# The first tree's masks by matrix products instead of a trip through DRAM, in a six-layer kernel on one core

## The chip, the cores and the metric

The kernel runs on one core of a Trainium2 chip. TensorE (PE) multiplies matrices, VectorE (DVE), ScalarE (ACT) and GpSimd (POOL) work on rows of 128 partitions, and SyncE (SP) does nothing but issue DMAs; ACT issues a few as well. Each engine runs its own list of instructions in order and waits on semaphores for the others. The time is the device time of one execution in microseconds: 1149.53 us, the median of three runs (1147.91 to 1149.95).

## The reference, cut to what matters

The input x holds 4 rows (batches) of 512 tokens with 128 features. Six layers follow each other, each with its own normalisation and a residual: a tree layer, causal attention with 16 heads, the tree layer again with the same weights, a mixture of 8 experts, a state-space block, and the mixture again. The change touches the first tree layer:

```python
x = x + 0.5 * _L0_ffn_ref(_layernorm(x, axis=-1), ...)

def _fff(x, node_w, node_b, w1, b1, w2, b2):     # once each for q, k and v
    for _ in range(DEPTH):                       # 4 levels, 16 leaves
        score = jnp.einsum('nd,nd->n', xf, node_w[cur]) + node_b[cur]
        cur = 2 * cur + 1 + (score >= 0).astype(jnp.int32)
    sel = jax.nn.one_hot(cur - N_NODES, N_LEAVES)
    hidden = jax.nn.relu(einsum('nd,ldh->lnh', xf, w1) + b1[:, None, :])
    hidden = hidden * sel.T[:, :, None]
    return einsum('lnh,lho->no', hidden, w2) + sel @ b2
```

Every token goes down a tree of 15 nodes and lands in one of 16 leaves; only that leaf's 64 hidden units count. The kernel computes all 1,024 hidden units of a tree for all tokens and multiplies them by a mask of 0 and 1. The three trees give q, k and v of an attention without heads over the 512 tokens of the row.

## The kernel before, in words

**Order of the work.** The table TIMES gives each job (layer letter and row: T0 to T3 are the first tree layer of rows 0 to 3, h0 to h3 the heads, and so on) due times for its preparation, its main part and its end. A loop takes the next step of the job that is due first; this gives the program order. A job that needs another one finishes that one first. The Tile framework then orders each engine's instructions itself, by the program order and its own estimate of when operands are ready, so an instruction without open operands can come long before its place in the program. Each role of tiles has a number of buffers (BUFS for SBUF, BANKS for the 8 banks of PSUM).

**A tree layer of one row.** `tree_prep` takes the statistics of the row's four blocks of 128 tokens (`stats`: L284 bn_stats and L286 bn_aggr for each block, then some 11 small DVE operations, L294, L271 to L277 three times over, L302, that make a reciprocal root; two of their operands lie in a PSUM bank of the role tree_tr). `layer_norm` applies them, on ACT for row 0 of the first layer (L310), else on POOL (L312). `features` turns the result around on PE (L318) and splits it into a rounded high part xh (ACT, L326) and a low part xl (DVE, L327); products of three partial matmuls (`mm3`, L173 to L175) then keep nearly full precision. The node scores become bits (DVE, L350), one matmul with the matrix leafpath (L353) counts the wrong turns on the way to each leaf, and "count equals 0" gives the one-hot choice: as bytes in `taken` (L355) and as numbers in `sel` (L369).

**Masks.** A chunk is 128 hidden units, two leaves of 64; a tree has 8 chunks. The mask of a tree is a tile of 128 partitions x 8 x 512 bytes in which each leaf's row of `taken` stands 64 times. It comes by DRAM: SP writes `taken` to the tensor fff_taken (L357), and after that has landed, two DMAs for each tree (L363) read the rows back, repeated. The role mask has 2 buffers.

**Main part.** `tree_main` runs over 24 chunks n (three trees of 8): three matmuls into a bank tree_mm (or start, for the odd chunks of row 0's first tree), one DVE operation L394 that adds the bias, cuts at zero and multiplies by the mask, and five chunks later the second matmul into tree_acc (L404, two instructions of TensorE for one product in full precision). L407 adds the leaf biases by `sel`. For row 0 the weights of the three trees are loaded and split on the way (`split_tree`): a stage DMA (L166), a rounded copy on ACT (L161), the remainder on DVE (first tree) or POOL (L162). `second_bias` (L230 to L240) folds the first bias into the second. The other rows fetch the split weights from DRAM.

**Around it.** `late_loads` (five attention weights, each a stage tile and an L161 and L162) is first in the program order. `head_consts` makes the constant rows of the heads: four stacks q_bias and two stacks k_bias of 128 x 1024, set to 1 by POOL (L480), then 24 rows overwritten from DRAM (L483, L484). Later `head_stack` and `head_maxima` move the q and k rows and the maxima of one pair of row and head group into the rows 24 to 127 of a stack of queries. `head_scores` runs over a quarter of the heads: a matmul (L557) and a DVE reduction (L565) for every tile.

Of the kernel before, what the change touches and what calls it, by code (L numbers as in the profile page):

```python
# [15 lines left out]
F32 = mybir.dt.float32  # L16
F32R = mybir.dt.float32r
# [4 lines left out]
ALU = mybir.AluOpType  # L22
AX = mybir.AxisListType

P = 128
B, S, D = 4, 512, 128
# [3 lines left out]
LEAVES, LEAF_W, DEPTH = 16, 64, 4  # L30
NODES = LEAVES - 1
NCH = LEAVES * LEAF_W // P
# [80 lines left out]
def macaron(ctx: ExitStack, tc: tile.TileContext, t: dict, stages: int = 6):  # L113
    nc = tc.nc
# [6 lines left out]
    def bank(role):  # L121
        return psum.tile([P, S], F32, tag=role, name=role, bufs=BANKS[role])
# [4 lines left out]
    def tiny(shape, tag, bufs=2):  # L127

        n = int(np.prod(shape[1:]))
        if tag not in turns:  # L130
            first = taken_of[0]
            taken_of[0] += bufs * n
            assert taken_of[0] <= SCRATCH
            turns[tag] = cycle([scratch[:, first + n * i : first + n * i + n] for i in range(bufs)])
        out = next(turns[tag])
        if len(shape) == 2:
            return out
        names = "abcd"[: len(shape) - 1]
        sizes = dict(zip(names, shape[1:]))
        return out.rearrange(f"p ({' '.join(names)}) -> p {' '.join(names)}", **sizes)  # L140

    def work(role, shape=(S,), dtype=F32):

        return wp.tile([P, *shape], dtype, tag=role, name=role, bufs=BUFS[role])
# [44 lines left out]
    x = [rows[:, b] for b in range(B)]  # L189
# [12 lines left out]
    leafpath, ident_h, future_t = (whole[:, ts(k, P)] for k in range(3))  # L202
    future = whole[:, 3 * P :]


    at = {}
    col = 0
# [59 lines left out]
    def inverse_root(out, v, s):  # L267

        shape = list(out.shape)
        y = tiny(shape, f"root_{shape[1]}", 4)  # L270
        nc.vector.tensor_scalar(  # L271
            y.bitcast(I32), v.bitcast(I32), -0.5, float(0x5F3759DF), ALU.mult, ALU.add
        )
        for k in range(3):
            nc.vector.scalar_tensor_tensor(s, y, -0.5, v, ALU.mult, ALU.mult)
            nc.vector.tensor_mul(s, s, y)
            nc.vector.scalar_tensor_tensor(out if k == 2 else y, s, 1.5, y, ALU.add, ALU.mult)  # L277

    def stats(b, role, square=False):

        st = tiny([P, NT, 6], "bn", 4)
        mv = tiny([P, NT, 2], "mv", 4)
        for i in range(NT):
            nc.vector.bn_stats(st[:, i, :], x[b][:, i, :])  # L284
        for i in range(NT):
            nc.vector.bn_aggr(mv[:, i, :], st[:, i, :])  # L286
        n = 2 if square else 1
        rstd, shift = (tiny([P, n, NT], f"{r}_{n}", 4) for r in ("rstd", "shift"))

        ps = bank(role)  # L290
        var, step = (
            ps[:, k * n * NT : (k + 1) * n * NT].rearrange("p (n t) -> p n t", n=n) for k in range(2)
        )
        nc.vector.tensor_scalar_add(var[:, 0, :], mv[:, :, 1], EPS)  # L294
        if square:

            nc.vector.scalar_tensor_tensor(
                var[:, 1, :], var[:, 0, :], EPS, mv[:, :, 1], ALU.mult, ALU.add
            )
        inverse_root(rstd, var, step)  # L300
        mean = mv[:, :, 0].unsqueeze(1).to_broadcast([P, n, NT])
        nc.vector.scalar_tensor_tensor(shift, mean, -1.0, rstd, ALU.mult, ALU.mult)  # L302
        return [(rstd[:, k, :], shift[:, k, :]) for k in range(n)]

    def layer_norm(b, rstd, shift, on_act=False, role="ln"):
        ln = work(role)
        for i in range(NT):
            out, by, to = ln[:, ts(i, P)], rstd[:, i : i + 1], shift[:, i : i + 1]
            if on_act:
                nc.scalar.activation(out, x[b][:, i, :], AF.Identity, scale=by, bias=to)  # L310
            else:
                nc.gpsimd.tensor_scalar(out, x[b][:, i, :], by, to, ALU.mult, ALU.add)  # L312
        return ln
# [25 lines left out]
        return tuple(w), second_weights(k)  # L339

    def tree_prep(b, st):
        ln = layer_norm(b, *stats(b, "tree_tr")[0], st.call == 0)
        yield
        st.xn = xn = features(ln, "tree_tr")
        yield

        ps = bank("tree_tr")
        mm3(ps, nodes, xn)
        bits = work("bits", dtype=BF16)
        nc.vector.tensor_scalar(bits, ps, at["node_b"], 0.0, ALU.add, ALU.is_ge)  # L350
        yield
        ps = bank("tree_tr")
        nc.tensor.matmul(ps, lhsT=leafpath, rhs=bits, start=True, stop=True)  # L353
        taken = work("taken", dtype=U8)[:ALL_LEAVES]
        nc.vector.tensor_scalar(taken, ps[:ALL_LEAVES], 0.0, None, ALU.is_equal)  # L355
        rows = t["fff_taken"][st.call]
        nc.sync.dma_start(out=rows, in_=taken)  # L357
        st.masks = []
        for k in range(TREES):
            mask = work("mask", (NCH, S), U8)  # L360
            pairs = rows[k * LEAVES : (k + 1) * LEAVES].rearrange("(c l) s -> l c s", l=2)
            for m in range(2):
                nc.sync.dma_start(  # L363
                    out=mask[m * LEAF_W : (m + 1) * LEAF_W],
                    in_=pairs[m : m + 1].to_broadcast([LEAF_W, NCH, S]),
                )
            st.masks.append(mask)
        st.sel = work("sel", dtype=F32R)
        nc.vector.tensor_scalar(st.sel, ps, 0.0, None, ALU.is_equal)  # L369

    def tree_main(b, st):
        xn = st.xn
# [101 lines left out]
    def head_consts():  # L474

        qs, ks = [], []
        for n, lst, name in ((4, qs, "q_bias"), (2, ks, "k_bias")):
            for u in range(n):
                stack = work(name, (2, S), F32R)
                nc.gpsimd.memset(stack.bitcast(F32), 1.0)  # L480
                for g in range(2):
                    raw = work("bias")
                    nc.sync.dma_start(out=raw[:R_HH], in_=t[name][u % 2, g])  # L483
                    nc.scalar.copy(stack[:R_HH, g, :], raw[:R_HH])  # L484
                lst.append(stack)

        vv = work("vv", (2, NT, V_COLS))
        nc.gpsimd.memset(vv, 0.0)
        by_head = vv[:, :, :, : HEADS * (HD + 1)].rearrange("p m n (h c) -> p m n h c", h=HEADS)
        for m in range(2):  # L490
            nc.gpsimd.memset(by_head[:, m, :, :, HD:], 1.0)
        return qs, ks, (vv, by_head)

    def head_prep(b, st, consts):
        all_qs, _, (_, by_head) = consts()
        st.qs = all_qs[b % 2 * 2 : b % 2 * 2 + 2]
        ln = layer_norm(b, *stats(b, "head_tr")[0])

        nc.gpsimd.tensor_add(x[b], x[b], out_b.unsqueeze(1).to_broadcast([P, NT, D]))
# [667 lines left out]
def _constants():  # L1167

    f = np.float32
# [46 lines left out]
    for q in range(GROUPS):  # L1216
# [10 lines left out]
        "lower": np.broadcast_to(lower, (P, EXPERTS, EXPERTS)),  # L1227
        "state_w": np.concatenate([np.zeros((P, 6, P), f), gather.reshape(P, 1, P)], axis=1),
        "spread": spread.reshape(P, GROUPS * P),
    }, head  # L1230


# [99 lines left out]
```

## Time and profile before

| what | value |
|---|---|
| median of three runs | 1149.53 us |
| profiled execution | 1150.85 us, span 1149.1 us |
| PE busy | 1080.6 us (94%) |
| DVE busy | 909.7 us (79%) |
| ACT, POOL busy | 517.1 us (45%), 411.6 us (36%) |
| PE busy in 0 to 12, 12 to 24, 24 to 29 us | 0.17, 10.15, 0.51 us |
| PE busy in 29 to 60 us | 31.0 us |
| PE busy in 200 to 400 us | 199.88 of 200 us |
| PE busy in 800 to 900 us | 85.76 of 100 us |

The profile is of one execution; it lists for each engine the busy time, and its views give the instructions in order of time, the waits with their releasers, and the chain of work that ended last. L with a number is a line of the kernel. A PE that is busy throughout can still be slow: the granted clock is listed beside it.

### The profile page before, as it was taken

To read this page: it belongs to the slowest core of one execution; us is meant where nothing else is said; L and a number is where in the kernel's file an instruction comes from. 1 tells how busy PE (TensorE), PEld (TensorE's weight loads), DVE (VectorE), ACT (ScalarE), POOL (GpSimd) and SP (SyncE) were. 2 spreads that over 40 slices of the span, in tenths; PEclk is the share of its full clock that TensorE was granted. 3 is DMA by queue.
4 is the path that set the end of the run, shared out by engine and by line. 5 is a ranking of instruction groups with operands and counts; after the bars stand their busy time and mean duration, and the time that the engine had idled before them with its cause. 6 is when DMAs were issued, how large, how long until landed. Compare 5 with 4: busy or idle time off the path is not lost.

```text
span 1149.1 us, 16519 instructions
## 1 busy us (share of the span) xinstructions
PE 1080.6 (94%) x5536; PEld 715.5 (62%) x5536; DVE 909.7 (79%) x2199; ACT 517.1 (45%) x1078; POOL 411.6 (36%) x396
## 2 busy tenths in 40 slices
PE   3999999999999999999999999998798989998998
PEld 2666566566665667765566676675276656655677
DVE  5566787577676677776789998799989999999864
ACT  2221423233332455544533643565476567454444
POOL 4115322002100141320314651266626656656623
PEclk9999999999999999999999999999899999999999
DMA  7787755231442122333752334662038323823310
GB/s 208 203 248 215 260 137 122 75 94 57 85 139 60 54 58 60 104 85 112 232 181 90 125 84 122 234 210 92 1 98 278 127 60 125 292 74 124 111 51 10
DMA packets 79653, 146.42 MB, mean 127 GB/s; under 512 B 7537, under 2 KB 39665, under 8 KB 79569
## 3 DMA queue, kind: packets, MB, share of 16 engines
q1 hardware_dynamic: 79280, 145.07, 42.1%
q8 instruction: 44, 0.72, 0.3%
q14 instruction: 41, 0.33, 0.1%
q10 hardware_dynamic: 288, 0.30, 0.1%
HBM read 125.35 MB, written 13.70 MB: 121 GB/s over the span
## 4 chain that ended last, share of the span: by engine, by line
PE 63%; DVE 20%; issue 6%; DMA 4%; POOL 3%; ACT 3%; SPq 1%; POOLq 0%; ACTq 0%; DVEq 0%
PE tree_acc L404 11%; PE moe_acc L773 7%; DVE states L972 6%; PE head_acc L601 5%; PE tree_mm L173 4%; PE head_max L557 4%; PE head_sc L633 3%; PE moe L173 3%; PE tree_mm L175 3%; PE tree_mm L174 3%; DVE states L971 3%; PE moe L174 3%; PE moe L175 3%; DVE u L759 2%; PE state_acc L934 2%
## 5 line engine op out<-in xcount | busy, mean ns | idle before, releaser
L973 POOL TENSOR_TENSOR states<-states,cs 128x512 f32<-128x512 f32 x128 | 163.4, 1282 | 161.9 <-DVE states L972 93.1
L404 PE MATMUL tree_acc<-full,ring 128*128 128x512 f32 x384 | 194.3, 598 | 5.2 <-DVE full L394 4.9
L565 DVE CUSTOM_DVE_ANT_0 head_max<-head_max,kept 128x128 f32<-128x128 f32 (+3 forms) x256 | 126.8, 496 | 64.1 <-PE head_max L557 61.9
L394 DVE SCALAR_TENSOR_TENSOR full<-tree_mm,kept,mask 128x512 f32<-128x512 f32 x188 | 138.5, 746 | 40.2 <-PE tree_mm L175 35.1
L649 ACT ACTIVATE pt<-head_sc 128x512 f32<-128x512 f32 (+1 forms) x176 | 95.0, 559 | 139.0 <-PE head_sc L641 138.3
L972 DVE TENSOR_TENSOR_SCAN states<-decay,states 128x512 f32<-128x512 f32 x128 | 154.6, 1216 | 0.5
L773 PEld LDWEIGHTS moe_acc<-ring,u 128*128 128x128 f32 x1152 | 141.4, 193 | 17.6 <-DVE u L765 3.0
L773 PE MATMUL moe_acc<-ring,u 128*128 128x128 f32 x1152 | 145.7, 278 | 1.0 <-DVE u L759 0.7
L173 PE MATMUL moe<-xl,ring 128*128 128x512 f32 x288 | 128.8, 448 | 8.9 <-DVE u L765 1.9
L784 POOL TENSOR_TENSOR kept<-kept,y 128x512 f32<-128x512 f32 x64 | 83.4, 1303 | 136.2 <-ACT y L783 118.8
L970 ACT ACTIVATE decay<-dts,kept 128x512 f32<-128x512 f32 x128 | 88.4, 693 | 88.1 <-DVE states L972 66.5
L758 ACT ACTIVATE u<-moe 128x512 f32<-128x512 f32 x144 | 86.3, 602 | 70.4 <-PE moe L175 66.5
L759 DVE SCALAR_TENSOR_TENSOR u<-u,moe 128x512 f32<-128x512 f32 x144 | 97.0, 677 | 23.4 <-ACT u L758 23.1
L174 PE MATMUL moe<-xh,ring 128*128 128x512 f32 x288 | 115.4, 401 | 0.0
L175 PE MATMUL moe<-xh,ring 128*128 128x512 f32 x288 | 115.0, 400 | 0.0
L541 POOL TENSOR_SCALAR km<-k_bias,kept 128x512 fp32r<-128x512 f32 x64 | 43.3, 697 | 171.3 <-PE head_sc L633 151.0
L783 ACT ACTIVATE y<-moe_acc,scratch 128x128 f32<-128x128 f32 x256 | 73.3, 370 | 65.6 <-PE moe_acc L773 64.8
L173 PE MATMUL tree_mm<-xl,ring 128*128 128x512 f32 x188 | 96.1, 514 | 0.4 <-DVE full L394 0.2
L404 PEld LDWEIGHTS tree_acc<-full,ring 128*128 128x128 f32 x384 | 71.0, 190 | 35.8 <-issue 17.3
L173 PEld LDWEIGHTS moe<-xl,ring 128*128 128x128 f32 x288 | 54.8, 190 | 60.4 <-DVE u L765 10.4
L557 PE MATMUL head_max<-km,q_bias 120*128 120x512 f32 (+2 forms) x192 | 91.7, 479 | 0.5 <-POOL km L541 0.4
L971 DVE TENSOR_TENSOR states<-state_b,dtxs 128x512 f32<-128x512 f32 x128 | 85.6, 682 | 5.5 <-PE state_acc L934 2.6
(242 smaller groups left out, 1982.3 us busy)
## 6 DMA issues: line engine op xcount, KB each, us to landing
ring<-moe_parts SPq DMA_DIRECT2D x72, 512.0 KB
ring<-tree_parts SPq DMA_DIRECT2D x42, 512.0 KB
ring<-in_fff_w SPq DMA_DIRECT2D x24, 512.0 KB
mask<-fff_taken SPq DMA_DIRECT2D x48, 256.0 KB
ring<-in_moe_w SPq DMA_DIRECT2D x16, 512.0 KB
dts<-state_rows SPq DMA_DIRECT2D x32, 256.0 KB
dtxs<-state_rows SPq DMA_DIRECT2D x32, 256.0 KB
moe_parts<-moe_w SPq DMA_DIRECT2D x9, 512.0 KB
```

The source lines that it names most:

```text
L173: nc.tensor.matmul(ps, lhsT=lh, rhs=rl, start=start, stop=False)
L174: nc.tensor.matmul(ps, lhsT=ll, rhs=rh, start=False, stop=False)
L175: nc.tensor.matmul(ps, lhsT=lh, rhs=rh, start=False, stop=stop)
L394: nc.vector.scalar_tensor_tensor(full, ps, neg_b1[:, n : n + 1], st.masks[k][:, c, :], ALU.max, ALU.mult)
L404: nc.tensor.matmul(acc, lhsT=weights[k][1][:, c, :], rhs=h, start=(c == 0), stop=False)
L557: nc.tensor.matmul(view, lhsT=qs[:R_MAX, g, ts(i, P)], rhs=km[j0 // 2][:R_MAX, j0 % 2 : j0 % 2 + each, :kw], start=True, stop=True,)
L565: nc.vector.tensor_tensor_reduce(view[:, n, :], view[:, n, :], future[:, S - kw :], -1.0, float(np.finfo(np.float32).max), ALU.add, ALU.mi ...
L759: nc.vector.scalar_tensor_tensor(u, u, 1.0, ps1, ALU.add, ALU.mult)
L773: nc.tensor.matmul(acc[:, ts(i, P)], lhsT=h[c][:, ts(i, P)], rhs=w2[:, e % 4 * 2 + c, :], start=(c == 0), stop=(c == 1),)
L971: nc.vector.tensor_mul(h, bs, dtx[:, g, :])
L972: nc.vector.tensor_tensor_scan(h, dA, h, 0.0, ALU.mult, ALU.add)
L973: nc.gpsimd.tensor_mul(h, h, cs[:, q])
```

## The change

- The mask of the first tree of row 0's first layer (call 0, tree 0) no longer comes by DRAM. A matrix leaf_rows of 16 x 1024, in which leaf l has ones over its 64 hidden units, is loaded by a DMA on ACT's queue at the start and rounded by a copy on ACT. For each of the 8 chunks one matmul of its 128 columns with the first 16 rows of `sel` gives the 128 x 512 mask in a bank tree_tr, and an ACT copy writes it as bytes. The two mask DMAs of that tree go; `taken`, its DRAM tensor and the masks of the other trees and rows stay. Both new tiles have the role stage.
- In call 0 `sel` is made before `taken`, in the other calls after, as it was.
- In the first layer of rows 1 to 3 the first bn_stats instruction is held, by `keep_in_program_order`, behind the instruction that precedes it on DVE in the program order. The other three bn_stats of a row are not held; all that needs the first one follows it.
- The four stacks q_bias are no longer set to 1 by POOL; the two stacks k_bias still are.

```diff
+    raw_rows, leaf_rows = (work("stage", [NCH * P], dt)[:LEAVES] for dt in (F32, F32R))
+    nc.scalar.dma_start(out=raw_rows, in_=t["leaf_rows"])
+    nc.scalar.copy(leaf_rows, raw_rows)
...
-    def stats(b, role, square=False):
+    def stats(b, role, square=False, late=False):
...
-            nc.vector.bn_stats(st[:, i, :], x[b][:, i, :])
+            first = nc.vector.bn_stats(st[:, i, :], x[b][:, i, :])
+            if late and i == 0:
+                tc.keep_in_program_order(first)
...
-        ln = layer_norm(b, *stats(b, "tree_tr")[0], st.call == 0)
+        ln = layer_norm(b, *stats(b, "tree_tr", late=0 < st.call < B)[0], st.call == 0)
...
+        st.sel = work("sel", dtype=F32R)
+        if st.call == 0:
+            nc.vector.tensor_scalar(st.sel, ps, 0.0, None, ALU.is_equal)
         taken = work("taken", dtype=U8)[:ALL_LEAVES]
         nc.vector.tensor_scalar(taken, ps[:ALL_LEAVES], 0.0, None, ALU.is_equal)
...
             mask = work("mask", (NCH, S), U8)
+            st.masks.append(mask)
+            if st.call == 0 and k == 0:
+
+                for c in range(NCH):
+                    ps_c = bank("tree_tr")
+                    nc.tensor.matmul(
+                        ps_c, lhsT=leaf_rows[:, ts(c, P)], rhs=st.sel[:LEAVES], start=True, stop=True
+                    )
+                    nc.scalar.copy(mask[:, c, :], ps_c)
+                continue
...
-            st.masks.append(mask)
-        st.sel = work("sel", dtype=F32R)
-        nc.vector.tensor_scalar(st.sel, ps, 0.0, None, ALU.is_equal)
+        if st.call:
+            nc.vector.tensor_scalar(st.sel, ps, 0.0, None, ALU.is_equal)
...
-                nc.gpsimd.memset(stack.bitcast(F32), 1.0)
+                if lst is ks:
+                    nc.gpsimd.memset(stack.bitcast(F32), 1.0)
...
+        "leaf_rows": np.kron(np.eye(LEAVES, dtype=f), np.ones((1, LEAF_W), f)),
```

## The prediction

> **What bounds the kernel now.** I read the page first: TensorE (PE) is busy 94% of the span, 31.0 of 31 us from 29 to 60 us and 199.88 of 200 us from 200 to 400 us. So where PE stands idle early, and nothing else is late, the end should move by nearly the same time. The waits of PE from 11 to 60 us name the two large ones:
>
> ```profile
> PE tree_tr L318 <- ACT ln L310: 11.8, 1, 11.8
> PE tree_acc L404 <- DVE full L394: 4.9, 1, 4.9
> ```
>
> (us in total, times, longest). The second is this change's place. The chain of work, in order of time (start, us, what), goes through it:
>
> ```profile
> 18.77 0.24 PE tree_tr L353
> 19.03 0.70 DVE taken L355
> 19.75 0.34 SPq L357
> 21.43 0.69 SPq L363
> 22.16 5.41 DMA mask<-fff_taken
> 27.69 0.76 DVE full L394
> 28.49 2.08 PE tree_acc L404 x2
> 33.51 2.58 PE tree_acc L404 x6
> 36.08 0.46 PE tree_mm L173 x2
> ```
>
> From the choice (19.03) to the first masked chunk (27.69) 8.7 us go into DRAM and back. PE has filled its six banks with chunks 0 to 5 and done the second bias by 23.55, then stands 4.94 us; tree 1 starts at 36.08. The windows (busy us per engine, granted clock, DMA share, GB/s) add that the pause also slows what follows it:
>
> ```profile
> 24.00:29.00 5.00, 0.51 (x1) 0.50 (x2) 2.50 (x9) 0.72 (x2) 1.78 (x4) 0.95 1.08 221
> 30.00:32.00 2.00, 2.00 (x5) 1.32 (x4) 1.84 (x4) 1.05 (x1) 0.79 (x1) 0.52 1.03 283
> ```
>
> The granted clock is 0.52 there. Between 28.49 and 32.81 two L404 take 2.08 instead of 0.86 us, three matmuls 0.43 instead of 0.23 each, two more L404 0.96: 1.92 us lost.
>
> The third view is the timeline (start, us): what stands before and behind the change.
>
> ```profile
> 0.73 3.62 POOL L480 MEMSET q_bias<- 128x1024 f32 x4 [0.29 <-POOLq L1309]
> 5.54 2.26 DVE L825 TENSOR_SCALAR kept<-kept 128x10 f32<-128x10 f32 x1
> 6.56 1.21 POOL L488 MEMSET vv<- 128x1336 f32 x1
> 9.44 1.22 DVE L162 TENSOR_TENSOR ring<-stage,ring 128x1024 fp32r<-128x1024 f32 x1
> 10.80 0.30 ACT L161 CAST attn_w<-stage 128x128 fp32r<-128x128 f32 x1 [1.65 <-DMA stage<-in_attn_w]
> 30.08 1.05 ACT L161 CAST ring<-stage 128x1024 fp32r<-128x1024 f32 x1 [5.36 <-DMA stage<-in_fff_w]
> 31.21 2.38 POOL L162 TENSOR_TENSOR ring<-stage,ring 128x1024 fp32r<-128x1024 f32 x1 [4.91 <-ACT ring L161]
> 128.79 0.21 DVE L294 TENSOR_SCALAR tree_tr<-scratch 128x4 f32<-128x4 f32 x1
> 141.58 0.70 DVE L565 CUSTOM_DVE_ANT_0 head_max<-head_max,kept 128x512 f32<-128x512 f32 x1 [0.16 <-PE head_max L557]
> 154.15 2.07 DVE L394 SCALAR_TENSOR_TENSOR full<-tree_mm,kept,mask 128x512 f32<-128x512 f32 x3
> ```
>
> **Masks by PE and ACT.** Removed: the pause of 4.94 us and the slow clock's 1.92, together 6.86. Added on PE: 8 matmuls of 512 columns at 0.23 us (L174 in the chain), 1.85 us. Left: 5.0 us, tree 1 at 31.1 instead of 36.08, if PE never waits. Can the masks keep up? `sel` is ready at 19.70, one matmul 0.39 (L353's span), one copy 0.59 (ACT's L326, same bank shape; a copy into bytes has no row, so 0.5 to 1.0), one L394 0.75: the first second-matmul can go at about 21.6, and PE still has the bias products until 23.55. ACT is idle from 18 to 22 us; eight copies take 4.8 us if two banks tree_tr alternate, 8.8 us (0.39 + 0.59 + 0.1 each) with one bank. PE's remaining work before tree 1 is 7.5 us behind 23.55, so even one bank, done by 28.5, hardly holds it. The bank is why the statistics matter: L294 of row 1 used one at 20.2 to 24.2.
>
> Next late: tree 1's weights. Their load was issued behind the two mask DMAs at 22.89 and landed at 30.08; copy and remainder end at 33.59. The removed DMAs are 0.5 MB; at 221 GB/s, the rate of that window with the DMA engines full, 2.3 us less in the queue. Against it `taken` comes 0.67 us later (`sel` goes first), which also delays the remaining masks' trip. Landing 28.3, remainder done 31.8, so PE's second matmul of tree 1 waits a few tenths. I take 4.5 us; the bounds are 2.5 (load not earlier: remainder at 33.6 against 36.1) and 5.0. The two new stage tiles take two of five buffers, leaf_rows until about 25 us; if tree 1's load had to wait for one, it would come no earlier than before, so that is the lower bound again.
>
> **Queries not preset, and the load of leaf_rows.** POOL loses 3.62 us of memsets, off the path. But DVE's L825 takes 2.26 us where its neighbour of the same kind (L823, 128x32) takes 0.17, and ends at 7.80, 0.03 us behind POOL's last memset: without the four sets ahead, POOL's remaining ones would end near 4.5 us and the 2 us of row 0's statistics go. They meet two later gates: DVE's order has the 1.22 us remainder L162 at 9.44, which needs ACT's copy that ends at 9.15, and ACT's order has the copy at 10.80, which waits for a DMA, ahead of row 0's normalisation at 11.28. I take 0.2 us gained; 2.1 if the new order moves both gates. On the other side the load of 64 KB (0.3 us at the first 12 us' 218 GB/s) and ACT's rounding of 1,024 columns (1.04, L161's row): 0.2 us lost, 1.3 at most if it lands in front of the normalisation. Sum 0, from -2.1 to +1.3.
>
> Here the skill would say more. The Trainium skill (SBUF — State Buffer, Who interferes with whom) says that a two-port DVE operation and a POOL instruction exclude each other for a whole instruction. By that alone the start would gain the 2.1 us; the trace's later gates decide, and leave 0.2.
>
> **Row 1's statistics.** By its due time (-1.4, when row 0's main part has made 11 steps) the first bn_stats is held behind L394 of chunk 10, before at 38.4 us, now about 34. The small chain of 12 operations at 0.2 us and POOL's L312 (1.78) end before 40. Row 1's transposes stood at 47.08 on PE, so about 42 now: hidden, 0. On DVE, busy 6.55 of 11 us from 29 to 40, 3 us fit.
>
> **Row 2's statistics.** This is the dangerous hold. Its preparation is forced by its main part's due time 79.5. Head h0's second group is then 10 of its 11 steps in: 16 + 14 reductions are traced, so row 2 is held behind the 30th L565. Counted on DVE's timeline that is the one at 141.58, where row 2's chain (L294 at 128.79, L302 at 136.96) ran after the 19th. After it come 0.5 us of statistics and 2.4 us of small operations alone, 8.8 when interleaved as before: ready at 145 to 152 instead of 137.6, 7.6 to 14 us late. Behind it wait POOL's L312, PE's transposes, `taken`, four mask DMAs on SP and the L394 at 154.15. What PE would miss: row 2's tree work, 4.55 + 2.04 = 6.6 us in 154 to 162. What fills it: the mixing of h0's second group, whose move of maxima sat between the two pairs of mask DMAs (issue 149.89, DMA share 1.08) and which began at 158.45; h1's statistics and projections, which shared a DVE that was 6.97 of 8 us busy, 4.27 of it row 2's. I take 1.0 us lost; the bounds are 1.1 gained (PE waited 1.13 us for a crowded DVE at 133 us, which row 2's operations leave) and 9.1 lost (all of its PE work in 154 to 168, 5.99 + 3.08, no filling). Row 3 is held behind the 40th L565 (152.99), its L294 was at 151.86: about 1 us, nothing.
>
> **Sum.** -4.5 + 0 + 0 + 1.0 = -3.5 us. Against the profiled execution (1150.85; span 1149.1 and 1.75 around it) that is 1147.35; the median of the runs is 1.32 us lower, so 1146.0. A difference under 0.2% (2.3 us) I call no change; more can be told.
>
> **Rivals.**
> - Tree 1's weights take the place of the masks. Speaking for it: ACT waited 5.36 us for that load. Against: 0.5 MB leave the queue. Gain 2.5, less 1.0: 1148.0, no change. Chance 0.12.
> - Row 2's masks late, the case on the other side. For it: DVE's order before had row 2 ahead of the 30th L565 by 12.8 us, and PE was busy 7.78 of 8 us there, so lost work isn't made good later. Against: the filling above. With no filling -4.5 + 9.1: 1154.1. It decides from 6.8 us of loss (4.5 + 2.3) on; between 2.2 and 6.8 it gives no change. Chance 0.32 for slower, 0.04 for no change.
> - The start's gates open too: -4.5 - 2.1 + 1.0: 1143.9. For it: the 2.26 us row. Against: both gates depend on loads that do not come earlier. Chance 0.10.
> - The masks don't speed anything, as one bank and copies of 1.0 us would give 1.5 us for each: the last at 31.7 instead of 25. PE's order could then wait about 2 us: included in the first rival's time.
>
> My forecast has 0.42. Faster 0.52, no change 0.16, slower 0.32. The range: from the gates with 5.0 instead of 4.5 and no loss at row 2 (1149.5 - 7.1 = 1142.4), and a little for orders of later work that move too, 1141.5; up to the slow rival, 1154. The forecast's own range is 1143.5 to 1147.2.
>
> **What would show it.** Right: PE's wait for L394 near 28 us gone, no granted clock near 0.5 after 20 us, tree 1's first L173 at 31 to 32, ACT's byte copies of 0.6 us from 20 us on, L825 at 0.2 us, row 2's L294 after 137 us (5 us earlier than 142). Wrong: a new wait on L161 or L162 of tree 1 over 2 us; PE idle more than 5 us between 140 and 165; or PE's idle time after 700 us, 41.8 of 449 us now by the windows, growing because the order there came out worse, which no row shows in advance.

## The result and the profile after

The changed kernel takes 1157.81 us (median of six runs, 1155.34 to 1162.29); the kernel before, in the runs beside it, 1149.03 us. The ratio is 1.0081, 95% interval [1.0058, 1.0105]: slower by 0.8%, where the forecast was 1146.0 and faster. The profiled execution of the changed kernel took 1155.34 us (span 1153.6), the fastest of the six.

The views of the changed kernel answer to those of before as follows. First the waits of PE from 10 to 40 us (us in total, times, longest):

```profile
PE tree_tr L324 <- ACT ln L316: 12.1, 2, 10.5
PE tree_tr L173 <- DVE xl L333: 1.4, 1, 1.4
```

The wait of 4.9 us for the first masked chunk is gone, as forecast, and nothing stands in its place. The window that held the pause and its slow clock (busy us per engine, granted clock, DMA share, GB/s):

```profile
24.00:29.00 5.00, 5.00 (x22) 3.03 (x22) 1.80 (x3) 2.94 (x5) 1.95 (x1) 1.00 1.08 297
```

PE is busy for 5.00 of 5 us instead of 0.51, at full clock. By these two views some 5 us should have been gained. The chain of work, in order of time (start, us, what), shows where they went:

```profile
20.25 0.23 PE tree_mm L175
20.48 0.66 PE tree_tr L375 x2
21.15 0.43 PE start L173
21.57 0.42 PE tree_tr L375
22.00 0.43 PE start L174
22.43 0.43 PE tree_tr L375
...
26.73 0.43 PE start L175
27.16 0.86 PE tree_acc L422 x2
```

L375 is the new leaf product. From the first of them on, each step takes 0.43 us: the leaf product, and also the main product behind it, which took 0.23 before (20.25). PE is never idle and does half the work. The timeline of PE's weight loads (start, us, what, and in brackets the idle time before it with its cause) says what has changed:

```profile
21.07 0.19 PEld L173 LDWEIGHTS start<-xl,ring 128*128 128x128 f32 x1 [0.37 <-issue]
21.50 0.18 PEld L375 LDWEIGHTS tree_tr<-sel,stage 16*128 16x128 f32 x1 [0.24 <-issue]
21.92 0.19 PEld L174 LDWEIGHTS start<-xh,ring 128*128 128x128 f32 x1 [0.24 <-issue]
```

Each load of 0.19 us starts 0.24 us after the one before has ended, at the start of its own product (21.50, 21.50): it isn't done behind the running product any more. What alternates is the shape, 16*128 and 128*128.

The second half of the story is row 2. In the timeline of DVE and SP:

```profile
141.85 0.70 DVE L584 CUSTOM_DVE_ANT_0 head_max<-head_max,kept 128x512 f32<-128x512 f32 x1 [2.61 <-PE head_sc L660]
...
142.47 0.29 DVE L288 BATCH_NORM_STATS2 scratch<-kept 128x6 f32<-128x128 f32 x1
...
143.01 0.17 DVE L300 TENSOR_SCALAR tree_tr<-scratch 128x4 f32<-128x4 f32 x1
...
157.35 2.66 SPq L382 DMA_DIRECT2D mask<-fff_taken  x4
```

The hold stands where the forecast put it, behind the 30th maximum, and the four mask DMAs go out at 157 us instead of 148.5 to 151. What that costs is best read from the closing product of each tree (L407 before, L425 after). The view of that line from 50 to 220 us gives the durations (ns, least, median and longest) and the starts of the first and the last: seven of them, from row 0's second tree to row 2's second. Before, then after:

```profile
L407 PE MATMUL tree_acc<-sel,rounded x7: 393/793/798, 59.2 to 207.9; 128*128 128x512 f32 x7
```

```profile
L425 PE MATMUL tree_acc<-sel,rounded x7: 393/793/800, 57.8 to 211.7; 128*128 128x512 f32 x7
```

At 58 us the changed kernel is 1.4 us ahead, at 212 us it is 3.8 behind; it has lost 5.2 us in between. From there on PE, DVE and ACT run the same instructions in the same order in both kernels, POOL from 239 us on, and PE's products stay 3.0 to 4.6 us late until 1,000 us. The windows from 138 to 168 us, before and after:

```profile
138.00:168.00 30.00, 28.77 (x169) 19.28 (x169) 23.92 (x91) 9.62 (x20) 9.11 (x18) 1.00 0.53 149
```

```profile
138.00:168.00 30.00, 27.89 (x163) 16.08 (x162) 20.22 (x94) 10.12 (x20) 7.83 (x15) 1.00 0.42 119
```

PE's busy time (first number) falls by 0.9 us, the time spent on loading weights (second) from 19.28 to 16.08 us. The busy time counts a slow pace in full. But not all of the fall in weight loads is lost work: another mix of products stands in this window. 46 of its 162 loads are now of 32 columns, 0.11 us each, where 30 of 169 were before; a load of 128 columns takes 0.19. Over the whole stretch between the closing products at 127 and 208 us the same 409 loads take 49.7 us before and 50.8 after. What holds PE up there is taken up again under row 2's hold.

### The profile page after: what moved, and what is told of

The parts are those of the page before. It is cut to its first block, busy times and chain, and to the rows that moved or that the text cites. A ratio compares the mean times of both kernels' runs of the same rounds, so it can differ in the third digit from the quotient of the medians.

```text
span 1153.6 us, 16553 instructions
## 1 busy us (share of the span) xinstructions
PE 1087.0 (94%) x5544; PEld 714.8 (62%) x5544; DVE 909.7 (79%) x2199; ACT 522.1 (45%) x1087; POOL 408.1 (35%) x392
## 4 chain that ended last, share of the span: by engine, by line
PE 63%; DVE 21%; issue 5%; POOL 4%; DMA 3%; ACT 3%; SPq 1%; POOLq 0%; DVEq 0%; ACTq 0%
PE tree_acc L422 12%; DVE states L991 7%; PE moe_acc L792 6%; PE head_acc L620 5%; PE tree_mm L173 4%; PE head_max L576 3%; PE moe L173 3%; PE head_sc L652 3%; DVE states L990 3%; PE tree_mm L175 3%; PE tree_mm L174 3%; PE moe L174 3%; PE moe L175 3%; DVE u L778 2%; DVE u L784 2%
## 5 line engine op out<-in xcount | busy, mean ns | idle before, releaser
L792 PEld LDWEIGHTS moe_acc<-ring,u 128*128 128x128 f32 x1152 | 140.2, 191 | 17.6 <-DVE u L784 3.0
L777 ACT ACTIVATE u<-moe 128x512 f32<-128x512 f32 x144 | 86.2, 601 | 67.9 <-PE moe L175 66.4
L174 PE MATMUL moe<-xh,ring 128*128 128x512 f32 x288 | 115.4, 401 | 0.0
L173 PEld LDWEIGHTS moe<-xl,ring 128*128 128x128 f32 x288 | 54.6, 190 | 63.0 <-DVE u L784 11.1
```

What stands on the lines that cost most here:

```text
L173: nc.tensor.matmul(ps, lhsT=lh, rhs=rl, start=start, stop=False)
L174: nc.tensor.matmul(ps, lhsT=ll, rhs=rh, start=False, stop=False)
L792: nc.tensor.matmul(acc[:, ts(i, P)], lhsT=h[c][:, ts(i, P)], rhs=w2[:, e % 4 * 2 + c, :], start=(c == 0), stop=(c == 1),)
```

## The experiments

All numbers on the traces are collected in one table; the sections below refer to it. "Tree 2" is the end of the closing product of row 0's second tree, "stage" the time from the closing product of row 1's third tree (127.2 us in the kernel before) to that of row 2's second, "rest" from there to the end of the span, "half clock" the total of the stretches with a granted clock of 0.5 (in each trace the last 1.6 to 3.5 us of it lie around the end of the span, where PE is done). The part left out, from tree 2 to row 1's third tree, is 67 to 68 us in all.

| kernel | tree 2 | stage | rest | half clock | median us | ratio to before [95%] |
|---|---|---|---|---|---|---|
| before | 60.0 | 81.4 | 940.4 | 30.3 | 1149.5 | |
| after | 58.6 | 86.3 | 941.0 | 19.9 | 1157.8 | 1.0081 [1.0058, 1.0105] |
| e8_again (after) | 61.3 | 86.2 | 939.2 | 15.9 | 1161.0 | 1.0094 [1.0058, 1.0130] |
| e1_row2_free | 60.3 | 82.1 | 943.2 | 33.0 | 1155.1 | 1.0049 [1.0031, 1.0067] |
| e2_holds_alone | 60.4 | 85.2 | 944.7 | 34.1 | 1159.5 | 1.0082 [1.0067, 1.0097] |
| e3_masks_alone | 58.8 | 81.4 | 943.0 | 26.4 | 1151.5 | 1.0017 [1.0003, 1.0030] |
| e4_queries_alone | 59.8 | 81.6 | 940.4 | 30.1 | 1151.8 | 1.0017 [1.0003, 1.0031] |
| e5_no_holds | 63.3 | 81.5 | 942.6 | 30.8 | 1155.3 | 1.0052 [1.0037, 1.0067] |
| e6_row23_hold | 61.5 | 85.5 | 943.4 | 33.3 | 1158.9 | 1.0074 [1.0046, 1.0102] |
| e7_row1_hold | 59.3 | 80.8 | 940.2 | 15.9 | 1150.9 | 1.0006 [0.9992, 1.0019] |
| e9_rows128 | 56.6 | 81.4 | 940.6 | 28.9 | 1145.4 | 0.9965 [0.9952, 0.9977] |
| e10_row2_hold | 60.7 | 87.4 | 941.7 | 27.4 | 1159.0 | 1.0080 [1.0055, 1.0105] |
| e11_row1_rows128 | 54.3 | 81.6 | 940.4 | 22.7 | 1145.7 | 0.9966 [0.9954, 0.9979] |
| e12_early_hold | 55.7 | 87.0 | 937.1 | 16.7 | 1150.5 | 1.0012 [0.9999, 1.0024] |
| e13_rows128_holds | 55.6 | 84.8 | 938.6 | 15.8 | 1148.6 | 0.9989 [0.9976, 1.0002] |
| e14_rows128_none | 55.2 | 81.0 | 941.4 | 19.2 | 1146.4 | 0.9976 [0.9964, 0.9988] |
| e15_mid_hold | 61.0 | 87.7 | 944.4 | 36.9 | 1160.9 | 1.0095 [1.0069, 1.0121] |
| e16_due_time_only | 55.6 | 84.1 | 941.3 | 30.5 | 1148.5 | 0.9991 [0.9981, 1.0002] |
| e17_early_stats | 56.2 | 81.3 | 939.4 | 23.2 | 1146.1 | 0.9963 [0.9950, 0.9977] |
| e18_stats_due_only | 55.0 | 86.0 | 939.7 | 19.0 | 1151.5 | 1.0019 [1.0009, 1.0030] |

### The parts, one at a time

Theory A: row 2's hold is the loss. Rival B: the masks by products, with the new order at the start, are.

**e1_row2_free**, the changed kernel with row 1's hold only:

```diff
-        ln = layer_norm(b, *stats(b, "tree_tr", late=0 < st.call < B)[0], st.call == 0)
+        ln = layer_norm(b, *stats(b, "tree_tr", late=st.call == 1)[0], st.call == 0)
```

> The changed kernel with the hold only on row 1; rows 2 and 3 have their statistics where the planner puts them, as before. Theory A (the held statistics of row 2 are what makes the changed kernel slow): the maxima and attention of 146 to 208 us no longer lose the 5 us that the two profiles show there (1.3 us ahead at 127 us, 3.9 behind at 208), row 2's first mask product stands near 153 us again, and the time is about 1152.5 (1157.8 minus 5.3), with tree 0 of row 2 starting 1 to 2 us earlier than in the kernel before. Rival B (the new order of the first 30 us is what every later order follows from, and the hold only happens to lie there): the time stays at 1156 to 1159 and the 5 us are still lost by 208 us.

The stage is back at 82.1 us, as A says, but the time only came to 1155.1, between the two: tree 2 ended at 60.3, no earlier than in the kernel before. So the start's gain wasn't there.

**e2_holds_alone**, the kernel before with the three holds:

```diff
-            nc.vector.bn_stats(st[:, i, :], x[b][:, i, :])
+            first = nc.vector.bn_stats(st[:, i, :], x[b][:, i, :])
+            if late and i == 0:
+                tc.keep_in_program_order(first)
...
+        ln = layer_norm(b, *stats(b, "tree_tr", late=0 < st.call < B)[0], st.call == 0)
```

> The kernel before with nothing but the three holds; masks by DRAM, queries preset. Theory A: row 2's first statistic goes behind the 30th maximum of h0's second group, near 141 to 142 us instead of 128, its masks come 8 to 9 us later, and the kernel takes about 5 us more than before: 1154. Rival B: within 2 us of the kernel before (1147 to 1151). Row 1's hold alone should cost nothing in either.

Stage 85.2 for 81.4, as expected; the time rose by more than the stage, to 1159.5.

**e3_masks_alone**, the changed kernel without holds and with the four presets put back:

```diff
-        ln = layer_norm(b, *stats(b, "tree_tr", late=0 < st.call < B)[0], st.call == 0)
+        ln = layer_norm(b, *stats(b, "tree_tr")[0], st.call == 0)
...
-                if lst is ks:
-                    nc.gpsimd.memset(stack.bitcast(F32), 1.0)
+                nc.gpsimd.memset(stack.bitcast(F32), 1.0)
```

> The changed kernel without any hold and with the queries' stacks preset again: what is left is the masks of the first tree by products and copies, with their load and its rounding. Theory A: the start's gain of 1.5 us that the profile of the changed kernel shows at 100 to 127 us stays, at most 2 us more or less, and nothing is given back at 208 us: 1146 to 1149. Rival B (masks and the new order at the start are the loss): 1152 to 1158. If row 1's statistics without a hold take one of the banks that the masks' products go through, the first tree ends later than in the changed kernel (its last product at 33.1 us before plus 1 to 2).

Neither: 1151.5. In its trace tree 2 is 1.2 us early, but the masks alone do not make the kernel faster.

**e4_queries_alone**, the kernel before without the four presets:

```diff
-                nc.gpsimd.memset(stack.bitcast(F32), 1.0)
+                if lst is ks:
+                    nc.gpsimd.memset(stack.bitcast(F32), 1.0)
```

> The kernel before without the four presets of the queries' stacks and nothing else. Both theories: DVE's 2.26 us row at the start falls to about 0.2, row 0's root is ready 1.3 us earlier (as in the changed kernel, 9.76 for 11.11), and the copy of the first attention weights on ACT, behind its load, may hold the normalisation; time from 1147.5 to 1149.5, that is 0 to 2 us gained. A loss over 2 us would say that the start's new order hurts by itself.

DVE's row fell from 2.26 to 0.14 us, and no milestone moved with it: tree 2 at 59.8, the end of the span 0.3 us later. The time, 1151.8, is 2 us above the kernel before where 0 to 2 below was expected, and the interval of the ratio leaves out 1; the trace does not show why.

**e5_no_holds**, as e3 with the presets left out, and **e8_again**, the changed kernel once more, look at the start:

```diff
-        ln = layer_norm(b, *stats(b, "tree_tr", late=0 < st.call < B)[0], st.call == 0)
+        ln = layer_norm(b, *stats(b, "tree_tr")[0], st.call == 0)
```

> The changed kernel without any hold: masks by products and copies, queries not preset, all rows' statistics where the planner puts them. Theory A (row 2's hold is the loss, the rest about nothing): attention of rows 1 to 3 passes 208 us within 1 us of the kernel before, and the time is 1147 to 1151. Theory C (row 1's hold costs as well, which is why the kernel with row 1 held alone stood at 1155): this one is 3 to 5 us below that, 1150 to 1152. Rival B (the masks and the new order at the start cost by themselves): 1153 to 1156.

> The changed kernel, nothing edited, for a second trace and further times. Its first trace was the fastest of six executions (span 1153.6 of 1153.6 to 1160.5). Expected: a median of 1155 to 1160; the loss between 127 and 208 us again 4.5 to 5.5, as the order is the same; and what the spread comes from, differences between the two traces in how many stretches of 3.41 us with a granted clock of 0.5 they have (5 in the first, 7 to 9 in the others seen), among them one at 24 to 33 us, which the first trace of the changed kernel alone did not have.

e5 came to 1155.3, as the rival B had it. With no hold at all its stage is 81.5 us. Its span is 5.7 us longer than before: 3.2 us of that lie at the start, where tree 2 ends at 63.3, and 2.2 in the rest. From e3 it differs by the presets alone, and it is 3.8 us slower. The chain of e5, then its windows:

```profile
23.06 0.43 PE start L175
23.49 0.64 PE tree_tr L375
24.13 0.72 PE tree_mm L173
24.86 0.72 PE tree_tr L375
...
30.05 3.41 PE tree_tr L238 x16
```

```profile
20.00:25.00 5.00, 5.00 (x13) 2.17 (x11) 3.38 (x6) 2.83 (x5) 0.00 (x0) 0.85 0.69 204
25.00:30.00 5.00, 5.00 (x9) 2.52 (x10) 0.75 (x1) 2.66 (x4) 0.00 (x0) 0.50 1.06 282
30.00:35.00 5.00, 5.00 (x22) 4.33 (x21) 2.43 (x11) 0.34 (x2) 2.36 (x1) 0.62 0.13 16
```

The alternating products run at 0.43 us, then the clock falls to a half for 10.24 us, although PE counts as busy throughout; the pitch becomes 0.72, and the 16 bias products take 3.41 instead of 1.78 us. So the pause was replaced by work at half pace, and PE's clock fell behind it as it had behind the pause. That the slow pace is the reason is not shown: the first trace of the changed kernel has the same pace and is the only one of the five traces with 16-row products without a half clock before 35 us; e1, e3 and e8 have one stretch of 3.41 us. In e8 the loss of the stage repeated to 0.1 us (86.2), while tree 2 came at 61.3 instead of 58.6. Its total of half clock was lower than expected (15.9 us), and it again was the fastest of its executions.

**e6_row23_hold**, **e7_row1_hold** and **e10_row2_hold** are e2 with a choice of rows:

```diff
+        ln = layer_norm(b, *stats(b, "tree_tr", late=1 < st.call < B)[0], st.call == 0)   # e6
+        ln = layer_norm(b, *stats(b, "tree_tr", late=st.call == 1)[0], st.call == 0)       # e7
+        ln = layer_norm(b, *stats(b, "tree_tr", late=st.call == 2)[0], st.call == 0)       # e10
```

> The kernel before with the holds of rows 2 and 3 alone. Theory A: the mixing of h0's second group moves ahead of row 2's products and runs without them between about 138 and 168 us, 4 us are lost by 208 us, and the time is 1154 to 1159, as with all three holds (1159.5). Theory C: about 4 us below that, as row 1's hold has its own price: 1154 to 1155.

> The kernel before with row 1's hold alone: its first statistic goes from before 20 us to behind the full of chunk 10 at about 38 us. Theory A: nothing, 1148.5 to 1151.5, and no milestone after 60 us moves by more than 0.7 us. Theory C: 3 to 5 us, 1153 to 1155, seen as a later second tree of row 1 at 60 to 100 us or in the states after 800 us.

> The kernel before with the hold of row 2 alone. Theory A: row 2's hold carries the whole price of the three (1159.5) and of rows 2 and 3 (1158.9): 4 us lost between 127 and 208 us, time 1157 to 1160. Rival: half of it or more comes from row 3's hold: 1151 to 1155.

The holds of rows 1 and 3 cost nothing (e7: 1150.9, interval across 1; e6 and e10 differ by 0.1 us). Row 2's hold alone carries the price of all three. Its closing products, for 59.2 to 207.9 before:

```profile
L409 PE MATMUL tree_acc<-sel,rounded x7: 392/793/798, 59.9 to 214.5; 128*128 128x512 f32 x7
```

### The leaf product's 16 rows

Theory D: the change of shape makes each of these products cost 0.43 us. Rival E: they wait for ACT's copies. **e9_rows128** is e3 with leaf products on all 128 rows; the rows below the 16 leaves are zero, so the masks are the same:

```diff
-    raw_rows, leaf_rows = (work("stage", [NCH * P], dt)[:LEAVES] for dt in (F32, F32R))
-    nc.scalar.dma_start(out=raw_rows, in_=t["leaf_rows"])
-    nc.scalar.copy(leaf_rows, raw_rows)
+    raw_rows, leaf_rows = (work("stage", [NCH * P], dt) for dt in (F32, F32R))
+    nc.gpsimd.memset(leaf_rows.bitcast(F32), 0.0)
+    nc.scalar.dma_start(out=raw_rows[:LEAVES], in_=t["leaf_rows"])
+    nc.scalar.copy(leaf_rows[:LEAVES], raw_rows[:LEAVES])
...
-                        ps_c, lhsT=leaf_rows[:, ts(c, P)], rhs=st.sel[:LEAVES], start=True, stop=True
+                        ps_c, lhsT=leaf_rows[:, ts(c, P)], rhs=st.sel, start=True, stop=True
```

> The masks alone, without holds and with all stacks preset, as the experiment on the masks alone (1151.5), but each leaf product takes 128 rows instead of 16: the rows below the 16 leaves are set to zero by one more operation of POOL, so the products' values are the same. Theory D (a product on 16 rows between products on 128 cannot load its weights behind the one before, so each of the 16 changes takes 0.43 instead of 0.23 us, 3.2 us in all): products from the first leaf product on follow each other at 0.23 us or wait for the copies, the clock is not halved between 20 and 30 us, tree 1 starts 1.5 to 3 us earlier, and the time is 1147.5 to 1150. Rival E (the products wait for the copies of ACT, 0.58 us each with a bank behind it, and the row count is nothing): pitch and time as with 16 rows, 1150.5 to 1152.5.

**e11_row1_rows128**, **e14_rows128_none** and **e13_rows128_holds** make the same edit in e1, in e5 and in the changed kernel itself:

> The changed kernel without the holds of rows 2 and 3, row 1 held as in the change, queries not preset, and the leaf products on 128 rows as above; beside it stands the same with 16 rows (1155.1). Theory D: 1.5 to 4 us less than that one, 1151 to 1153.5, with no stretch of half clock before 35 us. Rival E: 1154 to 1156.

> No hold, queries not preset, leaf products on 128 rows: beside it stands the same on 16 rows (1155.3, tree 0 and 1 done 3.3 us later than in the kernel before). Theory D: that loss came from the products' pitch of 0.43 us and the half clock that followed; tree 0's second tree now ends 3 to 6 us earlier than before, at 54 to 57 us, and the time is 1143 to 1147. Rival E: 1152 or more.

> The changed kernel with all holds where they are; only the leaf products take 128 rows. The sum of what was measured apart: row 2's hold costs 9 to 10 us of the time (1159.0 for 1148.8 to 1149.9), the start gains 3.5 us over the kernel before: 1153 to 1156. The stage from 127 to 208 us takes 85 to 87 us.

All four are faster than their twins with 16 rows: 1145.4 for 1151.5, 1145.7 for 1155.1, 1146.4 for 1155.3 and 1148.6 for 1157.8. The chain of e14, and its weight loads:

```profile
20.33 0.23 PE start L173
20.56 0.23 PE tree_tr L376
20.79 0.23 PE start L174
21.03 0.25 PE tree_tr L376
...
23.60 0.23 PE start L175
23.83 1.78 PE tree_tr L239 x16
```

```profile
19.94 0.19 PEld L173 LDWEIGHTS start<-xl,ring 128*128 128x128 f32 x1
20.19 0.19 PEld L376 LDWEIGHTS tree_tr<-sel,stage 128*128 128x128 f32 x1
20.40 0.19 PEld L174 LDWEIGHTS start<-xh,ring 128*128 128x128 f32 x1
```

The same alternation now goes at 0.23 us, and the weights of each product are loaded while the one before it runs. Theory E falls. No kernel with 128 rows has half clock before 35 us. Over all traces tree 2 ends at 60.4 us on average with masks by DRAM (seven kernels), at 60.5 with products on 16 rows (five) and at 55.5 on 128 rows (eight): the masks by products gain 4.9 us or nothing.

e13 came 4 to 7 us under what was expected of it, although its stage is the slow one (84.8): the prices of the two causes, taken from the times, do not add up.

### Why row 2's hold costs

Theory A in its sharper form: it costs by its lateness. Rival F: any hold costs. **e12_early_hold** (on e13) and **e15_mid_hold** (on e10) bring row 2's preparation forward by its due time, so that the hold lies behind the 18th and the 22nd maximum:

```diff
-    T2=(84.0, 94.3, 79.5, 137.6, 136.7, 159.9),
+    T2=(66.0, 76.3, 79.5, 137.6, 136.7, 159.9),     # e12; e15: 67.5, 77.8
```

> The changed kernel with all its holds and leaf products on 128 rows; only row 2's preparation has an earlier due time (66.0 for 84.0), so that its first statistic is held behind the 18th maximum of h0's second group and not the 30th. Theory A (what costs is how late row 2's chain starts, as the mixing then runs without products beside it): row 2's chain starts about 12 us earlier, near 129 us, the stage from 127 to 208 us takes 81 to 82.5 us again instead of 85 to 87, and the time is 1143.5 to 1147.5. Rival F (the hold costs wherever it lies, for it changes the order in which weights are loaded up to the end): 1149 or more.

> The kernel before with row 2's hold alone, by an earlier due time (67.5) behind the 22nd maximum instead of the 30th: about 9 us earlier, near 133 us. Theory A (price by lateness): row 2's chain starts about 4 us later than without a hold, hidden behind the attention of row 1: 1149.5 to 1153. Rival F (price of any hold): 1157 to 1160.

Both are against A: stage 87.0 and 87.7, times 1150.5 and 1160.9, though row 2's first masks were asked for at 142.3 and 148.2 us, no later than without a hold. But the due time had moved all steps of the preparation. **e16_due_time_only** is e12 without holds, **e17_early_stats**, with the holds, moves the first step alone (the second due time, 120.0, leaves the later steps to be drawn by the main part's 79.5, as before), and **e18_stats_due_only** is e17 without holds. Theory G: this stage's order is good at one place, and whatever moves row 2's chain off it costs.

```diff
-    T2=(84.0, 94.3, 79.5, 137.6, 136.7, 159.9),
+    T2=(66.0, 120.0, 79.5, 137.6, 136.7, 159.9),    # e17, e18; e16: 66.0, 76.3
```

> No hold at all, leaf products on 128 rows, queries not preset (twin: 1146.4, stage from 127 to 208 us 81.0 us), and only the due time of row 2's preparation as early as in the kernel whose hold lay behind the 18th maximum (stage 87.0). If that due time alone makes a worse order of the stage (theory G: the order of this stage is good at one place only, and whatever moves row 2's chain off it, earlier or later, costs): 84.5 to 88 us for the stage, time 1149 to 1152. If the hold did it (theory F): 81 to 82 us, 1145.5 to 1147.5.

> The changed kernel with all holds, leaf products on 128 rows (twin: 1148.6, stage 84.8 us): only the first step of row 2's preparation, its statistics and normalisation, has an earlier due time, so the hold lies behind the 18th maximum; the steps behind it are due as before. Theory A (lateness): the stage takes 81 to 82.5 us, time 1145.5 to 1147.5. Theories F and G: 84.5 to 88 us, 1148 to 1152.

> As the one before, without any hold: the due time of row 2's first step alone is moved. Theory A and theory F: stage 81 to 82 us, time 1145.5 to 1147.5 as its twin without holds (1146.4). Theory G: 84.5 to 88 us, 1148.5 to 1152, with row 2's chain of small operations earlier on DVE than 124 us.

e17 keeps all holds and loses nothing (81.3 us, 1146.1), so a hold by itself is free: F falls. e18 has none and loses 4.6 to 5 us (86.0, 1151.5): this is as G has it, and lateness is only one way of being off. e16, whose chain comes earliest, loses 2.7 to 3.1 us (84.1), a little less than G had it; a stretch of half clock of 3.41 us lies in its stage (from 163.7 us), in no other trace, and can be up to 1.7 us of that. Their closing products, e17 and then e18:

```profile
L426 PE MATMUL tree_acc<-sel,rounded x7: 393/793/798, 55.4 to 203.8; 128*128 128x512 f32 x7
```

```profile
L426 PE MATMUL tree_acc<-sel,rounded x7: 394/793/798, 54.2 to 207.3; 128*128 128x512 f32 x7
```

In e18 row 2's masks were asked for at 133.9 us, 11.7 us after row 1's last tree; in e16 at 128.8 (6.5 us after); in the ten traces that lose nothing 17.6 to 22.2 us after, and with the late hold (after, e2, e6, e8, e10, e13) 29.4 to 31.3. e12 and e15, with 19.4 and 20.0, do not fit this row, so the masks' time alone isn't the rule either.

What makes one order better by 4 us can in good part be read from the kept traces. The mixing of the heads (head_acc, L601 before, L620 after) multiplies with weights of 32 columns, 128*32, between products of 128*128. Behind their first two, such products of one group of heads stand on PE like this (start, us, what), before and then after:

```profile
140.05 1.06 PE L601 MATMUL head_acc<-pt,vv 128*32 128x512 f32 x8
151.14 0.85 PE L601 MATMUL head_acc<-pt,vv 128*32 128x384 f32 x8
152.35 0.85 PE L601 MATMUL head_acc<-pt,vv 128*32 128x256 f32 x14
```

```profile
138.34 1.05 PE L620 MATMUL head_acc<-pt,vv 128*32 128x512 f32 x4
139.77 1.04 PE L620 MATMUL head_acc<-pt,vv 128*32 128x512 f32 x2
142.12 0.83 PE L620 MATMUL head_acc<-pt,vv 128*32 128x384 f32 x2
146.81 0.85 PE L620 MATMUL head_acc<-pt,vv 128*32 128x384 f32 x8
148.67 0.63 PE L620 MATMUL head_acc<-pt,vv 128*32 128x256 f32 x6
151.46 0.42 PE L620 MATMUL head_acc<-pt,vv 128*32 128x128 f32 x8
```

In an unbroken run four of them start within 0.02 us, and the next four 0.3 to 0.5 us later. The step from a 128*32 product of 512 columns to one of 128*128 takes 0.52 us (median in e13, e14 and e18), from one 128*128 product of that length to the next 0.24. A run that is broken up pays the long step again. Between the two closing products the same 72 products come in 10 or 11 runs in the ten traces with a stage of 80.8 to 82.1 us, and in 13 to 16 runs in the ten with 84.1 to 87.7. The steps that begin at one of them take 8.3 us before and 11.1 after, 8.8 in e14 and 11.6 in e13 (PE's idle time left out). That is 2.8 us of the 4.9 and of the 3.9 us that the stage is longer. Part of the remainder is idle time of PE (1.0 us more after the change, none in e13). No run moved the mixing alone, so this is read from the traces and not tested.

Four versions beat both kernels: e9 (1145.4), e11 (1145.7), e14 (1146.4), and e17 (1146.1), which is the change with all its parts, its leaf products on 128 rows and row 2's first step due earlier.

## Why the prediction was wrong

**The masks, -4.5 forecast, about 0 measured.** What is removed was right: the pause is gone in every trace, its half clock in one of the five. The term that failed is "8 matmuls of 512 columns at 0.23 us (L174 in the chain)": L174's neighbours have its shape, a leaf product's have not. In the chain 13 steps take 0.43 instead of 0.23 us, 2.6 us, and behind them the clock fell again in four of five traces, up to 1.7 us lost for each stretch of 3.41. With the shape of L174 the term holds: tree 2 is 4.9 us earlier, and tree 1's first product stands at 29.03 us (e14) against 35.52 before and 32.35 after (forecast 31 to 32). A rule of the skill may bear on this and was not weighed: the Trainium skill (TensorEngine Tiling (Array Packing), Key Properties) says that changing the tiling mode drains TensorE. It does not say that a plain product on 16 rows counts as another mode; the rows here would fit that, at 0.2 us for each change of shape, but no run shows that a drain is the reason.

ACT's copies (0.58 us, forecast 0.6), the choice of `sel` first, and tree 1's weights not binding (PE waits for neither L161 nor L162) came as forecast. A rival named the masks as slow, but by the copies and one bank, which no run shows. (Its sum for one bank is slightly off: 8 copies of 0.39 + 0.59 + 0.1 us make 8.6, not 8.8; nothing hangs on it.)

**Queries not preset, 0 forecast.** In e4's trace 0 came (tree 2 at 59.8 for 60.0), by the mechanism forecast, later gates. In the times it was not 0: 2.0 us lost in e4, where the bound was 1.3, and 3.8 us between e3 and e5, whose trace has them at the start (tree 2 at 63.3 for 58.8); on 128 rows e14 is only 1.1 us above e9, within the noise. What costs there is not shown. The timeline of the changed kernel:

```profile
6.04 0.14 DVE L844 TENSOR_SCALAR kept<-kept 128x10 f32<-128x10 f32 x1
...
9.94 1.26 ACT L316 ACTIVATE ln<-kept,scratch 128x128 f32<-128x128 f32 x3 [3.31 <-DVE scratch L308]
11.48 1.04 ACT L161 CAST ring<-stage 128x1024 fp32r<-128x1024 f32 x1 [0.28 <-DMA stage<-in_fff_w]
12.44 0.49 ACT L161 CAST attn_w<-stage 128x128 fp32r<-128x128 f32 x2
12.83 0.49 ACT L316 ACTIVATE ln<-kept,scratch 128x128 f32<-128x128 f32 x1
```

The statistics come 1.3 us earlier, but ACT's order has the copy of tree 0's weights ahead of the fourth block. SP's order had put rows 1 to 3 of x and the bias before that load, which landed at 11.46 instead of 8.1 us. The gate forecast was another one, the attention weights' copy. The row of 2.26 us fell to 0.14 in e4, with nothing but the presets gone, which fits the rule that the prediction cites (the Trainium skill, SBUF — State Buffer, Who interferes with whom); the 2.1 us that this would have gained at the end did not come.

**Rows 1 and 3, 0 forecast:** right (e7; e6 against e10).

**Row 2, +1.0 forecast, bounds -1.1 to 9.1.** Measured in the stage: 85.9 on average in the six traces with the late hold (after, e8, e2, e6, e10, e13) against 81.4 in the nine without it and with the old due times, +4.5. The place of the hold, its lateness (L300 at 143.0, masks at 157.4) and the filling were right: the mixing of h0's second group moved ahead, its first 16 products to 162.0 to 167.1 us from 172.4 to 184.9. The step that failed is that this filling costs 1.0. It took the room in pieces: the mixing's 72 products come in 14 runs instead of 10, and the steps at them take 2.8 us more. The sign set for it, PE idle for more than 5 us from 140 to 165 us, did not show (27.89 of 30 us busy): PE loses most of this time while it counts as busy, and only 1.0 of the stage's 4.9 us by standing idle. The rival with row 2's masks late stood on the right side, with 1154.1, still 3.7 us short of the time measured.

**The sum.** In the traces: start between 1.4 us gained and 1.3 lost, stage 4.8 to 4.9 lost, which makes the spans 4.5 and 5.2 us longer (after, e8). The times differ by 8.8. Part of the rest is the choice of execution: both traces are the fastest of their set, and the kernel before's own trace is 1.3 us above its median. The six times of the changed kernel rise as their granted clock falls, from 1155.3 us at 0.992 to 1162.3 at 0.987. Why row 2's hold costs 9 to 10 us of the time in e2, e6 and e10, and only 2.1 between e13 and e14, is not settled. In the traces of e2 and e6 4.4 and 3.0 us of it stand in the rest behind 208 us, where PE, DVE and ACT keep one order, in e10 1.3.

## What to carry to other kernels

- A small product put between large ones is priced by its neighbours. Where the number of rows changes, look at the weight loads: if the load starts with its own product, fill the operand with zero rows until the shapes agree. Here that made the difference between nothing and 4.9 us gained at the second tree.
- Where a pause is filled with dependent work, ask at what pace it is filled. PE's busy time does not show it; the times of one product that both kernels have do. Weight loads per window do so only where the windows hold the same products.
- An order worked out by a planner can be good at one place only. Moving one chain by 10 us, earlier or later, cost 3 to 6 us here, most of it without a new wait. Look at what the move breaks up, here the runs of 128*32 products; bound it by the whole of the work in reach, and try it at more than one place.

## What the runs showed of the hardware that was not expected

- Products of 16*128 between products of 128*128 take 0.43 us each, and so do the 128*128 ones behind them; with 128*128 throughout they take 0.23 (after and e14). The step from a 128*32 product of 512 columns to one of 128*128 takes 0.52 (e13, e14, e18).
- The stretches of half clock are 3.41 us long or a multiple (3.41, 6.83, 10.24), but for the last one around the end of each trace, and their position against the start of the program differs between executions of the same kernel. The Trainium skill (TensorE: Matmul & The Clock Gate, Part 1: The HAM clock gate) gives a free-running window of 3413 ns, which agrees. Each costs up to 1.7 us, and the traces hold 15.8 to 36.9 us of them, most behind 795 us. The four traces with 33 us or more took 943.2 to 944.7 us for the rest behind 208 us, the four with less than 17 us 937.1 to 940.2. So a single execution of this kernel can't settle a difference of 2 or 3 us.
- The clock falls to a half while PE counts as busy without a gap, where its products had followed each other at 0.43 instead of 0.23 us (e5, from 23.5 us); in the first trace of the changed kernel, at the same pace, it did not fall.
